# Splitting the context again in two stages instead of storing its high and low halves

## The chip, the cores and the metric

The kernel runs on one core of a Trainium2 chip. The metric is the device time of one execution in microseconds (us). TensorE (PE, with its weight loads shown as PEld), VectorE (DVE), ScalarE (ACT) and GpSimd (POOL) each take their instructions in order; SyncE (SP) issues every DMA of this kernel, also in order.

## The reference, cut to what matters

Four transformer layers run one after the other on `x` (32 batches of 112 tokens by 256 channels). Every layer attends from `x` to the same context `ctx_1024` (32 batches of 375 tokens by 256 channels). Layer 0 normalises the context first; layers 1, 2 and 3 project it raw:

```python
x = _L0_xattn_ref(x, ctx_1024, ...)             # cross attention, context rms-normalised
x = _L1_xattn_ref(x, ctx_1024, ...)             # self attention, cross attention, gated feed-forward, 8-bit rounding
    k = (ctx @ wk) ; v = (ctx @ wv)
x = _L2_xattn_ref(x, ctx_1024, ctx_1024, ...)   # cross attention, 16 heads of 64, feed-forward
    K = einsum('bsc,hdc->bhsd', k, Wk) ; V = einsum('bsc,hdc->bhsd', v, Wv)
x = _L3_xattn_ref(ctx_1024, x, ...)             # causal self attention, cross attention to x_e = ctx, feed-forward
    k = einsum('btc,hcd->bhtd', kv_in, wk) + bk ; v = ...
```

Everything is float32. The kernel gets float32 accuracy from faster matmuls by splitting an operand into a high half (rounded to the float32r type) and a low half (the rest), and adding three products: high by high, high by low, low by high.

## The kernel before, in words

**Stages.** The nine sweeps over the 32 batches are named layer and kind: `l0x`, `l1s`, `l1x`, `l1f`, `l2x`, `l2f`, `l3s`, `l3x`, `l3f` (s self, x cross, f feed-forward). They run in five stages: l0x beside l1s, l1x beside l1f, l2x alone, l2f beside l3s, l3x beside l3f. A batch is 8 slots long in l1x and l2x (one slot is two heads in l1x, and one pair of heads of one quarter in l2x) and 4 slots in l3s (four heads each); groups of two batches share the norm, the query projection and, in l3s, the keys.

**The order.** `run` writes the instructions out slot by slot. What belongs to a slot comes with a lag in slots (`LAGS`): in l2x the scores and softmax in the slot itself, the normalising of the probabilities one slot later, their transposes two, the product with the values three. What prepares a unit is an atom with a lead in slots (`LEAD`): an atom of cost 0 (a load, a split) is written when its slot comes, projections fill in by their cost. The compiler's scheduler then orders each engine's instructions from that list by a simulated time; on the chip each engine follows its own list in order, and waits where something is not ready.

**Buffers.** SBUF tiles come from pools with a fixed number of buffers: `k3` has 11, shared by raw context, values, probabilities, transposed probabilities, keys and projected halves; `k6` has 5, for the split context (high and low, 128 x 2 x 2 x 376) and, in l3s, for the keys read back.

**The context.** `ctx_atoms` (L530) serves l1x and l2x. In l1x, `load` (atom `cload`) takes a k3 tile, clears its last column on POOL (L540) and loads 375 KB of raw context (L541); `cut` takes a k6 tile and calls `split` (L228): a copy of 128x752 into the high half, on ACT or DVE in turn as `SHARE` says (L200, L202), and a subtraction on POOL into the low half (L231). As l1x is not the last sweep, `cut` then stores the two halves in DRAM (`cd`, 752 KB, L552). From then on `kept(b)` finds them: in l2x `load` does nothing and `cut` loads 752 KB from `cd` into a k6 tile (L547). In l3s, `kv_atoms` (L508) already projects the context with the weights of l3x: its `load` (atom `c2`, L516) loads 752 KB from `cd`, `qk_atoms` projects the keys, `v_atoms` the values, both with lead 1, and both go to DRAM (L842, L521) for l3x.

**What stands around it in SP's order.** l1x has four DMA transposes per batch (L1125), which turn the rounded probabilities for the matmuls of L1070. l2x loads values projected earlier (L750) and turns its queries by four DMAs (L681). l3s writes its queries and keys to DRAM (L868, L842) and reads them back spread out: two keys tiles (L852) and eight query DMAs per batch (L879), which the scores of L1158 wait for.

Of the kernel before, what the change touches and what calls it, by code (L numbers as in the profile page):

```python
# [8 lines left out]
F32 = mybir.dt.float32  # L9
F32R = mybir.dt.float32r  # L10
# [9 lines left out]
TE = 376  # L20
# [41 lines left out]
class Kern:  # L62
# [7 lines left out]
        l1x=[0, 1, 3, 6, 7],  # L70
        l1f=[0, 1, 5, 0, 3],
        l2x=[0, 1, 2, 3, 3],
        l2f=[0, 0, 0, 0, 0],
        l3s=[0, 0, 1, 2, 2],
# [6 lines left out]
        l1s=dict(load=5, stats=5, apply=3, q=2, k=2, v=1),  # L81
        l1x=dict(load=17, stats=12, apply=10, cload=14, cut=14, q=8, apart=[2, -1], k=4, v=-1, v2=[-2, -4, -6, -7], again=-7),
        l1f=dict(load=13, stats=11, apply=10, gate=2, gelu=1, again=-3),
        l2x=dict(load=10, stats=7, apply=6, cload=11, cut=7, q=4, k=[1, 1], v=0, vload=2),
        l2f=dict(load=6, stats=5, apply=3),
        l3s=dict(load=10, stats=8, apply=7, q=7, qload=3, k=6, v=3, c2=4, k2=1, v2=1),
        l3x=dict(load=16, stats=11, apply=10, cload=13, cut=12, q=9, qload=4, k=8, v=6, kload=8, vload=4),
        l3f=dict(load=6, stats=5, apply=2),
    )
# [152 lines left out]
    def vec(self, name, ncol):  # L242
# [12 lines left out]
        l3s="L3_xattn_m_proj_b", l3x="L3_xattn_c_proj_b", l3f="L3_xattn_f_b2",  # L255
# [218 lines left out]

        return [(L["load"], 0, load), (L["stats"], 0, stats), (L["apply"], gb * 200, apply)]

    def kept(self, b):
        return self.cd.get(b)

    def early_v(self, qd):  # L480

        return qd < self.EARLY and "l1x" in self.sweeps and "l2x" in self.sweeps
# [25 lines left out]
    def kv_atoms(self, s, b, wd, kb):  # L508

        nc = self.nc  # L510
        L = self.LEAD[s]
        st = {}

        def load():
            st["c"] = o = self.t([128, 2, 2, TE], F32R, "k6")
            nc.sync.dma_start(o.bitcast(F32), self.kept(b).bitcast(F32))  # L516

        def keep_v(v):
            d = self.v3[b] = self.dram([2, TB, 768], F32, f"v3_{b}", 1)
            for q in range(2):  # L520
                nc.sync.dma_start(d[q], v[q].rearrange("p a h d -> p (a h d)"))  # L521

        blocks = [(a * TB, TB) for a in range(3)]
        return (
            [(L["c2"], 0, load)]
            + self.qk_atoms(L["k2"], lambda: wd["k2"], lambda: lambda k, q: st["c"][:, k, q, :], TE, False, False, kb, None, f"k3_{b}", lambda d: self.k3.update({b: d}))
            + self.v_atoms(L["v2"], lambda: wd["v2"], lambda k, q, a: st["c"][:, k, q, a * TB : (a + 1) * TB], blocks, None, None, keep_v)
        )

    def ctx_atoms(self, s, b, c):  # L530


        nc = self.nc
        L = self.LEAD[s]

        def load():
            if self.kept(b) is not None:
                return
            c["raw"] = raw = self.t([128, 2, TE], F32, "k3")
            nc.gpsimd.memset(raw[:, :, T:TE], 0.0)  # L540
            nc.sync.dma_start(raw[:, :, :T], self.A["ctxT"][b].rearrange("(k p) t -> p k t", p=128))  # L541

        def cut():
            c["c"] = o = self.t([128, 2, 2, TE], F32R, "k6")
            d = self.kept(b)
            if d is not None:
                nc.sync.dma_start(o.bitcast(F32), d.bitcast(F32))  # L547
                return
            self.split(c["raw"], o[:, :, 0, :], o[:, :, 1, :], ("ctx", "crest"))
            if s != self.sweeps[-1]:  # L550
                d = self.dram([128, 2, 2, TE], F32R, f"cd{b}", 1)
                nc.sync.dma_start(d.bitcast(F32), o.bitcast(F32))  # L552
                self.cd[b] = d

        return [(L["cload"], 0, load), (L["cut"], 0, cut)]

    def ctx_norm_atoms(self, s, b, g, c):

# [802 lines left out]
    OVER = dict(l2x=0.0, l3x=34.0)  # L1361

    def run(self):
        self.xd, self.cd, self.vd, self.k3, self.v3, self.mark = {}, {}, {}, {}, {}, {}
        ws = {s: self.weights(s) for s in self.sweeps}
        units = {}
        for s in self.sweeps:
# [24 lines left out]
        for s in self.sweeps:  # L1392
            n, at = 0, []
            for u in units[s]:
                for q, (lead, cost, f) in enumerate(u.atoms):
                    m = n - lead
                    d = mine[s][m] if 0 <= m < len(mine[s]) else mine[s][0] + m if m < 0 else mine[s][-1] + m - len(mine[s]) + 1
# [84 lines left out]
        for k in range(max(max(due), len(slots)) + 1):  # L1482
# [7 lines left out]
            if k < len(slots):  # L1490
                s, ui, sl = slots[k]
# [18 lines left out]
            for q in range(1, 5):  # L1510
                for j in [j for e, j in due.get(k, []) if e == q]:
                    self.cur = slots[j][0]
                    f = slots[j][2].st[q]
# [81 lines left out]
```

## Time and profile before

| what | value |
|---|---|
| median of 3 runs | 4973.1 us (4965.27 to 4977.62) |
| the profiled execution's own time | 4961.83 us |
| its span in the trace | 4960.0 us |
| l0x and l1s | about 0 to 1116 us |
| l1x and l1f | about 1116 to 2232 us |
| l2x | about 2232 to 3348 us |
| l2f and l3s, with the changes of stage around them | about 3348 to 4216 us |
| l3x and l3f | about 4216 to 4960 us |
| stores of halves (cd<-k), all in l1x | 32 of 752 KB |
| loads of halves (k<-cd), 32 in l2x and 32 in l3s | 64 of 752 KB |
| loads of raw context, all in l1x | 32 of 375 KB |

In the profile, L12 is line 12 of the kernel; `k` stands for any tile of the pools k3, k6 and ki, and buffer numbers are left out. An idle time carries the name of what ended it ("<-DMA k<-cd": a load from cd landed). "PEclk" or "granted clock" is the share of TensorE's clock that the chip granted. A line of `copy` or `split` is shared by many callers, so the shape tells which one it is: 128x752 is the context.

### The profile page before, as it was taken

To read this page: it belongs to the slowest core of one execution; us is meant where nothing else is said; L and a number is where in the kernel's file an instruction comes from. 1 tells how busy PE (TensorE), PEld (TensorE's weight loads), DVE (VectorE), ACT (ScalarE), POOL (GpSimd) and SP (SyncE) were. 2 spreads that over 40 slices of the span, in tenths; PEclk is the share of its full clock that TensorE was granted. 3 is DMA by queue.
4 is the path that set the end of the run, shared out by engine and by line. 5 is a ranking of instruction groups with operands and counts; after the bars stand their busy time and mean duration, and the time that the engine had idled before them with its cause. 6 is when DMAs were issued, how large, how long until landed. Compare 5 with 4: busy or idle time off the path is not lost.

```text
span 4960.0 us, 111607 instructions
## 1 busy us (share of the span) xinstructions
PE 4515.7 (91%) x37824; PEld 4007.3 (81%) x37824; DVE 3631.7 (73%) x9806; ACT 3417.2 (69%) x10644; POOL 2110.2 (43%) x3674
## 2 busy tenths in 40 slices
PE   6999999998779888888999999998999986899999
PEld 5888888886668777777999999998888875788888
DVE  4788888888887777776688888886555554777776
ACT  4788888887777776675577777774555544677776
POOL 4455555555443333332233333334333332556655
PEclk9999999999889999999999999999999997999999
DMA  4433333335676666676454555443665666666662
GB/s 102 124 84 86 84 81 84 86 84 132 138 148 134 131 134 134 132 147 132 112 142 143 143 143 143 142 132 109 206 192 177 205 191 192 171 159 160 161 160 77
DMA packets 585414, 674.53 MB, mean 136 GB/s; under 512 B 318688, under 2 KB 495056, under 8 KB 584656
## 3 DMA queue, kind: packets, MB, share of 16 engines
q1 hardware_dynamic: 584848, 667.40, 53.3%
q8 instruction: 305, 5.00, 0.4%
q14 instruction: 261, 2.14, 0.1%
HBM read 323.55 MB, written 173.02 MB: 100 GB/s over the span
## 4 chain that ended last, share of the span: by engine, by line
PE 39%; DMA 7%; DVE 4%; ACT 1%; SPq 1%; issue 1%; POOL 1%; ACTq 0%; DVEq 0%; POOLq 0%
PE ps L664 6%; PE ps L235 5%; PE ps L236 4%; PE ps L237 4%; PE sc L773 3%; PE ps L795 3%; PE ps L1070 3%; DMA qs<-dq_l3s 2%; PE sc L1106 2%; PE acc L235 1%; PE acc L237 1%; DMA k<-cd 1%; PE acc L236 1%; PE ps L1233 1%; PE acc L1273 1%
## 5 line engine op out<-in xcount | busy, mean ns | idle before, releaser
L217 POOL TENSOR_SCALAR k<-k,sm 112x375 f32<-112x375 f32 (+1 forms) x1536 | 928.7, 617 | 1051.7 <-DVE sm L646 475.9
L200 ACT ACTIVATE k<-ps 125x336 f32<-125x336 f32 (+4 forms) x2005 | 912.4, 468 | 418.8 <-PE ps L237 194.9
L606 DVE TENSOR_REDUCE sm<-sc 112x1 f32<-112x375 f32 x1792 | 947.0, 540 | 177.0 <-PE sc L773 88.9
L612 ACT ACTIVATE k<-sc,sm 112x375 f32<-112x375 f32 x1536 | 878.2, 577 | 106.7 <-DVE sm L606 86.6
L664 PE MATMUL ps<-ident,k 112*125 112x112 f32 x4608 | 730.2, 276 | 17.4 <-issue 4.2
L664 PEld LDWEIGHTS ps<-ident,k 112*125 112x125 f32 x4608 | 649.0, 189 | 69.9 <-issue 36.3
L773 PE MATMUL sc<-k,qs 128*112 128x376 f32 x2048 | 540.9, 357 | 18.0 <-ACT k L612 9.0
L235 PE MATMUL ps<-w,k 128*125 128x256 f32 (+2 forms) x1344 | 433.4, 322 | 33.1 <-ACT k L612 17.5
L235 PE MATMUL ps<-h,w 128*128 128x224 f32 x1408 | 409.4, 297 | 42.5 <-DVE h L202 15.9
L695 DVE TENSOR_TENSOR k<-ps,k 64x376 fp32r<-64x376 f32 x640 | 350.1, 547 | 121.5 <-ACT k L200 106.2
L236 PE MATMUL ps<-h,w 128*128 128x224 f32 x1408 | 393.4, 282 | 0.5 <-DVE h L231 0.5
L202 DVE COPY k<-ps 125x336 f32<-125x336 f32 (+2 forms) x619 | 289.2, 467 | 141.2 <-PE ps L237 71.7
L237 PE MATMUL ps<-h,w 128*128 128x224 f32 x1408 | 391.5, 281 | 0.0
L236 PE MATMUL ps<-w,k 128*125 128x256 f32 (+2 forms) x1344 | 389.6, 290 | 0.0
L237 PE MATMUL ps<-w,k 128*125 128x256 f32 (+2 forms) x1344 | 388.9, 289 | 0.0
L235 PE MATMUL ps<-k,w 128*128 128x376 f32 x896 | 343.8, 384 | 41.6 <-DMA k<-cd 28.7
L213 POOL TENSOR_SCALAR k<-k,sm 112x375 f32<-112x375 f32 x256 | 164.4, 642 | 448.4 <-DVE sm L646 279.4
L795 PE MATMUL ps<-k,k 125*64 125x112 f32 (+1 forms) x4608 | 350.7, 296 | 2.1 <-ACT k L200 1.3
L773 PEld LDWEIGHTS sc<-k,qs 128*112 128x112 f32 x2048 | 304.8, 177 | 47.0 <-ACT k L612 23.6
L235 PEld LDWEIGHTS ps<-h,w 128*128 128x128 f32 x1408 | 272.3, 196 | 69.7 <-issue 20.2
L235 PEld LDWEIGHTS ps<-w,k 128*125 128x125 f32 (+2 forms) x1344 | 263.5, 196 | 73.6 <-ACT k L612 28.2
L612 ACT ACTIVATION_READ_ACCUMULATOR k<-sc,sm 112x1 f32 x1536 | 321.1, 209 | 0.0
(213 smaller groups left out, 12642.2 us busy)
## 6 DMA issues: line engine op xcount, KB each, us to landing
qs<-h SPq DMA_DIRECT2D x512, 224.0 KB
k<-k SPq DMA_DIRECT2D x192, 376.0 KB
k<-cd SPq DMA_DIRECT2D x64, 752.0 KB
vd<-k SPq DMA_DIRECT2D x128, 375.0 KB
k<-vd SPq DMA_DIRECT2D x128, 375.0 KB
qs<-dq_l3s SPq DMA_DIRECT2D x256, 112.0 KB
qs<-dq_l3x SPq DMA_DIRECT2D x256, 112.0 KB
x<-xd SPq DMA_DIRECT2D x224, 112.0 KB
```

What stands on the lines that cost most here:

```text
L200: self.nc.scalar.activation(out, in_, AF.Identity)
L202: self.nc.vector.tensor_copy(out, in_)
L217: self.nc.gpsimd.tensor_scalar(out, in_, by, 1.0, ALU.mult, ALU.mult)
L235: mm(out, lhs(0), rhs(0), start=start, stop=False)
L236: mm(out, lhs(0), rhs(1), start=False, stop=False)
L237: mm(out, lhs(1), rhs(0), start=False, stop=stop)
L606: nc.vector.tensor_reduce(nms[j], sc[j][:, :n], AX.X, ALU.max, negate=True)
L612: nc.scalar.activation(p[:, j, :n], sc[j][:, :n], AF.Exp, bias=nms[j], scale=1.0 if scale is None else scale, accum_out=sm[:, j : j + 1])
L664: self.nc.tensor.transpose(pst[:TB, a * S : (a + 1) * S], p[:, j, a * TB : (a + 1) * TB], self.ident[:S, :S])
L695: nc.vector.tensor_tensor(ks[o, j, :], pk[r, :TE], ks[r, j, :].bitcast(F32), ALU.subtract)
L773: nc.tensor.matmul(sc[:, :TE], qs[:, hd, q, bs], kk, start=q == 0, stop=q == 1)
L795: nc.tensor.matmul(o if gqa else o[:, mm, :], vq[:, a, hd * 64 : hd * 64 + 64], st["pt"][:, :, j, ta] if gqa else st["pt", mm][:, j, ta], ...
```

## The change

The halves are no longer stored. `kept` and the dictionary `cd` go. `ctx_atoms` always loads raw context and always splits it; it now takes the names of its two leads, and `kv_atoms` in l3s uses it in place of its own load. So l1x loses its store; l2x and l3s each load 375 KB into a k3 tile in place of 752 KB into a k6 tile, and split it. In l2x the load moves from lead 7 (there it was part of `cut`) to lead 9 and the split has lead 7; in l3s the load moves from lead 4 to lead 5 and the split has lead 4. The copy into the high half is on ACT in l2x, on ACT and DVE in turn in l3s; the subtraction is on POOL in both.

```diff
-        l2x=dict(load=10, stats=7, apply=6, cload=11, cut=7, q=4, k=[1, 1], v=0, vload=2),
+        l2x=dict(load=10, stats=7, apply=6, cload=9, cut=7, q=4, k=[1, 1], v=0, vload=2),
-        l3s=dict(load=10, stats=8, apply=7, q=7, qload=3, k=6, v=3, c2=4, k2=1, v2=1),
+        l3s=dict(load=10, stats=8, apply=7, q=7, qload=3, k=6, v=3, c2=5, cut2=4, k2=1, v2=1),
...
-        ("l1x", "ctx"): (1, 1, 0),
+        ("l1x", "ctx"): (1, 1, 0), ("l2x", "ctx"): (1, 0, 0), ("l3s", "ctx"): (1, 1, 0),
...
-    def kept(self, b):
-        return self.cd.get(b)
...
     def kv_atoms(self, s, b, wd, kb):
...
-        def load():
-            st["c"] = o = self.t([128, 2, 2, TE], F32R, "k6")
-            nc.sync.dma_start(o.bitcast(F32), self.kept(b).bitcast(F32))
...
         return (
-            [(L["c2"], 0, load)]
+            self.ctx_atoms(s, b, st, ("c2", "cut2"))
             + self.qk_atoms(L["k2"], ...)
             + self.v_atoms(L["v2"], ...)
         )
-    def ctx_atoms(self, s, b, c):
+    def ctx_atoms(self, s, b, c, leads=("cload", "cut")):
...
         def load():
-            if self.kept(b) is not None:
-                return
             c["raw"] = raw = self.t([128, 2, TE], F32, "k3")
             nc.gpsimd.memset(raw[:, :, T:TE], 0.0)
             nc.sync.dma_start(raw[:, :, :T], self.A["ctxT"][b].rearrange("(k p) t -> p k t", p=128))

         def cut():
             c["c"] = o = self.t([128, 2, 2, TE], F32R, "k6")
-            d = self.kept(b)
-            if d is not None:
-                nc.sync.dma_start(o.bitcast(F32), d.bitcast(F32))
-                return
             self.split(c["raw"], o[:, :, 0, :], o[:, :, 1, :], ("ctx", "crest"))
-            if s != self.sweeps[-1]:
-                d = self.dram([128, 2, 2, TE], F32R, f"cd{b}", 1)
-                nc.sync.dma_start(d.bitcast(F32), o.bitcast(F32))
-                self.cd[b] = d
-
-        return [(L["cload"], 0, load), (L["cut"], 0, cut)]
+
+        return [(L[leads[0]], 0, load), (L[leads[1]], 0, cut)]
```

More of the change, by code (lines that the diff above doesn't have):

```diff
@@ L1363, in run @@
     def run(self):
-        self.xd, self.cd, self.vd, self.k3, self.v3, self.mark = {}, {}, {}, {}, {}, {}
+        self.xd, self.vd, self.k3, self.v3, self.mark = {}, {}, {}, {}, {}
         ws = {s: self.weights(s) for s in self.sweeps}
```

## The prediction

> **What bounds the kernel now.** I read the busy times by stage first, then the waits inside the three stages that the change touches, then the order of time around their DMAs. The table by stage (span, then busy time of PE, PEld, DVE, ACT and POOL, granted clock, DMA share, GB/s):
>
> ```profile
> 1116.00:2232.00 1116.00, 939.05 (x7027) 812.48 (x7024) 888.22 (x2462) 795.46 (x2243) 442.62 (x720) 0.93 0.67 137
> 2480.00:3348.00 868.00, 864.29 (x7691) 816.03 (x7690) 712.66 (x1665) 628.01 (x1782) 281.41 (x477) 1.00 0.50 141
> 3472.00:4216.00 744.00, 646.46 (x5319) 582.29 (x5317) 394.31 (x1092) 371.44 (x1510) 267.06 (x459) 0.92 0.63 194
> ```
>
> PE bounds l2x: 3.7 us idle in 868, at full clock. In l1x (first line) it is idle for 177 of 1116 us and in l3s (third) for 98 of 744, both at a lower clock and with more DMA. So work taken from the DMAs can pay in l1x and l3s, and nothing but PE's own work counts in l2x.
>
> l3s, in order of time: SP around one group's loads, and PE's first matmul after them; then its waits in the stage.
>
> ```profile
> 3620.05 1.53 SPq L516 DMA_DIRECT2D k<-cd  x1
> 3621.64 3.59 SPq L879 DMA_DIRECT2D qs<-dq_l3s  x4
> 3625.32 0.49 SPq L516 DMA_DIRECT2D k<-cd  x1
> 3626.75 12.53 SPq L879 DMA_DIRECT2D qs<-dq_l3s  x8
> 3634.16 0.65 PE L235 MATMUL ps<-k,w 128*128 128x376 f32 x1 [5.95 <-DMA k<-cd]
> ...
> PE sc L1158 <- DMA qs<-dq_l3s: 35.0, 13, 7.9
> PE ps L235 <- DMA k<-cd: 26.6, 6, 9.4
> ...
> SPq L879 <- DMA k<-cd: 49.9, 24, 2.8
> ```
>
> Two kept loads and 12 query loads go out in one burst of 2 x 752 + 12 x 112 = 2848 KB, and PE waits for its last pieces. In the timeline of PE this comes once per group of two batches, some 46 us apart: 13 waits from 3540 to 4098 us, of 1.29, 4.37, 5.95, 0.99, 2.05, 3.53, 3.62, 2.58, 3.03, 1.46, 4.75, 3.90 and 9.37 us, 46.9 us in all. Each ends 11.9 to 16.0 us after one kept load was issued and 7.5 to 11.4 us after the next; 4 end on `cd`, 9 on query loads behind it. SP is itself held at L879 until `cd` loads have landed.
>
> The clock after such a wait (same columns as the table):
>
> ```profile
> 3634.10:3637.60 3.50, 3.44 (x16) 2.53 (x16) 1.19 (x4) 0.00 (x0) 0.00 (x0) 0.50 0.71 200
> 3637.60:3641.10 3.50, 3.50 (x19) 3.50 (x18) 2.79 (x10) 0.00 (x0) 0.00 (x0) 0.50 0.38 114
> ...
> 1865.00:1868.50 3.50, 3.46 (x22) 3.09 (x22) 1.61 (x4) 1.80 (x6) 0.00 (x0) 0.54 1.77 196
> ```
>
> The clock is halved for 3.5 to 7 us after a wait of 2 to 6 us, so a wait costs about 1.7 us more than its length (3.5 x 0.5).
>
> l1x, one batch in order of time:
>
> ```profile
> 1858.00 4.26 SPq L1125 DMA_TRANSPOSE k<-k  x1
> 1859.08 1.80 POOL L231 TENSOR_TENSOR k<-k,k 128x752 fp32r<-128x752 f32 x1 [2.04 <-DVE sm L646]
> 1862.32 0.73 SPq L552 DMA_DIRECT2D cd<-k  x1
> 1865.04 0.47 PE L1070 MATMUL ps<-k,k 128*32 128x112 bf16 x12 [2.09 <-DMA k<-k]
> ```
>
> The store of the halves goes out 0.06 us after a transpose has been issued, and PE waits for that transpose. Of PE's 70 us of waits on transposes from 1240 to 2232 us, 50.4 us (24 waits, 2.1 us each) have a store between the transpose and its use; the 18 others are 1.1 us each. From the end of the transpose's issue to its use it is 3.54 us with a store, 3.01 us without.
>
> Prices of what is added, from l1x, where all of it runs already:
>
> ```profile
> L231 POOL TENSOR_TENSOR k<-k,k 128x752 fp32r<-128x752 f32 x32 | 59.3, 1852 | 54.7 <-DVE sm L646 22.5 <-ACT k L200 18.7 <-DVE k L202 13.5
> L200 ACT ACTIVATE k<-k x16: 818/831/865, 1111.5 to 2178.8; 128x752 fp32r<-128x752 f32 x16
> L540 POOL MEMSET k<- 128x2 f32 x31 | 5.3, 172 | 0.8 <-DMA k<-k 0.8
> ```
>
> The DVE copy of the same shape takes 0.55 us.
>
> **The change part by part.** *l1x loses 32 stores.* SP gets back 0.68 us of issue each, off the path: SP waits at most of its instructions. On the path is the delay of the transpose in flight. By landing times it is 0.53 us x 24 = 13 us; by the sizes of the waits, 1.0 us x 24 = 24 us. I take 18 us between them. At worst it is 0, if what makes those transposes late is the split on POOL before them, which stays; at best all 50 us, and 20 of clock. The split itself and L541 do not change.
>
> *l2x loads raw context and splits it.* Per batch POOL gets 1.85 + 0.17 us and ACT 0.83 us in about 34 us of a batch; they are busy 281 and 628 of 868 us there. What covers it is the lag of one slot, some 4.3 us, between normalising on POOL and the transposes on PE, against a delay of at most 2.0 us. The load is off the path: issue to copy is 3.2 to 8.3 us in l1x, against two slots (8.6 us) between the leads. Two things are queued behind: on POOL, the normalising (L217) behind the clearing and the subtraction; on ACT, the exponentials and key copies behind the copy. New is a buffer: raw context holds one of 11 k3 buffers for some two slots, and l2x's value loads already wait for one (SP at L750 for scores, 170.6 us in 62 waits). A value load has six slots before its use, so I take 0.25 us per batch, 8 us. Ends: a gain of at most 4 us (PE's idle time); a loss of all that is added in a row, 2.85 us x 32 = 91 us, if there is no cover. I stay near the low end as the nearest row is PE's 3.7 us of idle beside POOL's hundreds. SP's own waits at L547 (113.5 us, for a free k6 buffer) go; nothing late hangs on them.
>
> *l3s loads raw context and splits it.* The burst shrinks to 2 x 375 + 12 x 112 = 2094 KB, 26% less; 14 us of it are 3.7 us less. Each of the 13 waits loses that, or all it has: 37 us. Nine of them vanish and take their slow clock along: 9 x 1.7 = 15 us. Together 52 us. What is late next is the projection's own list: PE fills 86% of the stage, and the gaps that remain are of 1 us (on L202 and L926). Ends: 24 us, if only the waits on `cd` go (23.7 us); 47 + 13 x 1.7 + 8 = 77 us, if all go with some at the stage's end. Added are 0.83 us on ACT or 0.55 us on DVE, and 2.02 us on POOL per batch of 23 us, where they are busy 371, 394 and 267 of 744 us. The copy now waits in order for its load, with softmaxes queued behind it on ACT and normalisings on POOL. In l1x, where load and split have the same lead, that costs 13 us in 31 loads (8.6 on DVE, 4.6 on ACT); here a slot lies between. I take 0.2 us per batch on the path, 6 us. Ends: 0, and 2.5 us x 32 = 81 us with no cover.
>
> The sum is -18 + 8 - 52 + 6 = -56 us: 4961.8 becomes 4906 for the profiled execution. That one is 11.3 us below the median of the runs; from the median, 4973.1 becomes 4917 us.
>
> **Two rules of the Trainium skill.** For the loads, the row is 11.9 to 14.1 us from issue to use of a kept half against 3.2 to 8.3 us for raw context. "DMA: Bandwidth & Descriptors" (Anatomy of one DMA) gives about 2.0 us plus bytes by 436 GB/s, measured on the other descriptor path: by it a load would fall only from 3.8 to 2.9 us, and the l3s part would be worth 32 x 0.9 = 28 us rather than 52. For the clock, the row is a granted clock of 0.54 after a wait of 2.09 us. "TensorE: Matmul & The Clock Gate" (Part 1) has the clock fall only after an idle window of about 3.4 us: by it, short waits would cost no clock, and of the 15 us only the two vanishing waits of over 3.4 us would count, 3 us.
>
> **The rivals.** *The wait is handed on.* The query loads and the value stores keep the burst's length (SP is held at L879 for 64.9 us by v<-k, more than by `cd`), so l3s gains 12 us, l1x nothing, and the 14 us added remain: 4973 + 2 = 4975. For it: 9 of 13 waits end on queries. Against it: all 13 come with two kept loads.
>
> *l2x starves for k3 buffers.* Raw context takes a buffer, probabilities and keys wait, and PE, which has no idle time to give, loses the full 2.85 us per batch: 4973 - 18 - 52 + 91 + 6 = 5000. It makes the kernel no faster from 2.0 us of stall per batch on (64 us) and slower by the bound from 2.5. For it: the value loads' waits. Against it: these loads are early by design, and a k3 buffer comes free every 1.2 us or so (3.5 k3 tiles per slot of 4.3 us).
>
> *ACT and DVE wait for late raw loads in l3s.* SP stays late and a load takes 12 us; the copy stands a slot (5.8 us) behind, holds its engine for 6 us, and a quarter of that reaches PE in place of today's waits: 32 x 1.6 = 51 us, 4973 - 18 + 8 + 51 = 5014. Against it: a landing of about 4 us in l1x at a higher DMA share.
>
> *The burst dissolves.* The load goes out a slot earlier, all of the 77 us come, and l1x gives 40 with clock: 4973 - 77 - 40 + 8 + 6 = 4870.
>
> **How the numbers follow.** Chances: forecast 0.60, handed on 0.15, starved 0.13, late loads 0.07, dissolved 0.05. The forecast's own range is 4885 to 4950. Reaching to the other cases, 4868 to 4995 leaves out half of each extreme. A measurement tells 0.3%, 15 us, from no change. Faster: 0.60 + 0.05 + a fifth of the handed-on case = 0.68; the rest of that case 0.12; slower 0.20.
>
> **What would show it.** No cd<-k and no k<-cd; 96 raw loads of 375 KB; 96 subtractions of 128x752 on POOL. In l3s PE's waits on query loads below 20 us in all, none over 4 us on context, and a clock above 0.95 over the stage. In l1x, PE's waits on transposes at 45 to 57 us. In l2x PE idle below 15 us. It is wrong if l2x is longer by more than 20 us, if ACT, DVE or POOL show long waits on in_ctxT in l3s, or if the once-per-group wait stays with its size.

## The result and the profile after

The changed kernel takes 5019.07 us (median of 6 runs, 5015.54 to 5020.8), the kernel before 4975.36 us beside it (6 runs, 4965.27 to 4981.68). The ratio is 1.0074, with a 95% interval of 1.0057 to 1.009: slower, where the prediction said 4917 us and faster. The profiled execution has a span of 5017.5 us, that of before 4960.0.

The first and last value stores (vd<-k) and l3s's query loads (qs<-dq_l3s) mark the stages in SP's order of time, in every kernel of this study. l1x is from the first vd<-k to the last, l2x from there to the first qs<-dq_l3s, l3s from there to the last row of them (a row can hold several loads, and its start counts). Each stage time is of one profiled execution, and executions differ: beside e5 to e8, the kernel before took 4962 to 5010 us.

| us | to l1x | l1x | l2x | l3s | rest | span |
|---|---|---|---|---|---|---|
| before | 1168.4 | 1143.0 | 1132.7 | 743.5 | 772.4 | 4960.0 |
| after | 1172.8 | 1158.0 | 1155.2 | 754.3 | 777.2 | 5017.5 |

Of the 57.5 us, 15.0 lie in l1x, 22.5 in l2x and 10.8 in l3s. The 15 of l1x are within its spread. Seven experiments below have l1x as before had it, and take 1159.3, 1163.7, 1157.0, 1153.6, 1157.3, 1146.5 and 1157.8 us for it; with the 1143.0 of before, the shortest, the mean is 1154.8. Five have l1x as after has it, and take 1148.2, 1158.7, 1159.8, 1164.4 and 1154.4 us; with the 1158.0 of after the mean is 1157.3. The medians of the runs are 43.7 us apart: l2x and l3s make up 33 of them, and the rest has no place in these profiles.

The table by stage of the changed kernel (span, then busy time of PE, PEld, DVE, ACT and POOL, granted clock, DMA share, GB/s); the second and third stretch are moved by 30 and 38 us against those shown of before, roughly as the work is:

```profile
1116.00:2232.00 1116.00, 934.42 (x6976) 804.79 (x6975) 881.29 (x2445) 789.24 (x2226) 438.30 (x717) 0.92 0.58 112
2510.00:3378.00 868.00, 849.80 (x7495) 795.02 (x7495) 705.83 (x1621) 632.01 (x1762) 328.06 (x520) 1.00 0.47 127
3510.00:4254.00 744.00, 644.40 (x5227) 576.49 (x5226) 405.99 (x1087) 373.06 (x1496) 315.62 (x511) 0.92 0.58 175
```

The DMAs did get lighter: 0.67 to 0.58 in l1x, 0.63 to 0.58 in l3s. PE got nothing for it. In l2x it does 7495 matmuls in 868 us where it did 7691, and is idle for 18.2 us instead of 3.7.

*l1x.* PE's waits on transposes, 70.4 us (41 waits) before from 1240 to 2250 us, are nearly what they were (over the whole stage 78.6 us before and 79.0 after):

```profile
PE ps L1052 <- DMA k<-k: 68.3, 37, 8.0
```

*l2x.* ACT's waits (total, times, longest) from 2510 to 3378 us:

```profile
ACT k L200 <- DMA k<-in_ctxT_dram: 30.9, 22, 2.9
```

and one of them in order of time, on SP, ACT and POOL:

```profile
2967.40 0.93 SPq L531 DMA_DIRECT2D k<-in_ctxT_dram  x1
...
2972.78 0.83 ACT L200 ACTIVATE k<-k 128x752 fp32r<-128x752 f32 x1 [1.95 <-DMA k<-in_ctxT_dram]
2973.52 0.52 ACT L211 ACTIVATE xh<-ps,vec_L_xattn_ln_b,vec_L_xattn_ln_w 128x224 f32<-128x224 f32 x1
...
2973.69 1.78 POOL L231 TENSOR_TENSOR k<-k,k 128x752 fp32r<-128x752 f32 x1 [1.37 <-ACT k L200]
```

The load goes out 5.4 us ahead of its copy and lands just then. ACT stands for 1.95 us, the scaling of xh (L211) behind it is late, and POOL waits too. Further down the line PE waits for what DVE makes of that xh, a wait that before did not have, and the longest in total of PE's 18.2 us of idle time:

```profile
PE ps L777 <- DVE xh L213: 5.3, 5, 1.8
```

SP issues the load late because the k3 tile comes late: it waits at L531 for the matmuls (L777) that give a tile back.

```profile
SPq L531 <- PE ps L777: 40.9, 14, 3.4
```

*l3s.* One group in order of time, on SP, DVE, POOL, ACT and PE:

```profile
3964.20 0.46 SPq L531 DMA_DIRECT2D k<-in_ctxT_dram  x1
...
3969.35 0.55 DVE L202 CAST k<-k 128x752 fp32r<-128x752 f32 x1 [5.56 <-DMA k<-in_ctxT_dram]
...
3969.98 1.77 POOL L231 TENSOR_TENSOR k<-k,k 128x752 fp32r<-128x752 f32 x1 [5.76 <-DVE k L202]
...
3970.16 0.28 ACT L200 ACTIVATE k<-ps 125x128 f32<-125x128 f32 x1 [4.50 <-DVE k L202]
3970.33 0.54 ACT L200 ACTIVATE pp<-ps 112x448 f32<-112x448 f32 x1
...
3970.92 0.84 PE L1052 MATMUL ps<-pp,s 112*32 112x112 f32 x8 [3.10 <-ACT pp L200]
```

The six lines are one chain. The load lands 5.15 us after its issue. DVE stands before the copy in order; a part of the value projection is to be copied behind it; ACT, which copies the next part into the same tile, waits for DVE; the probabilities (pp) are queued behind that on ACT; PE waits for the probabilities. Over the stage, from 3520 to 4160 us:

```profile
PE ps L1052 <- ACT pp L200: 21.4, 12, 3.5
PE sc L1140 <- DMA qs<-dq_l3s: 21.1, 11, 3.5
ACT k L200 <- DMA k<-in_ctxT_dram: 31.9, 12, 4.8
DVE k L202 <- DMA k<-in_ctxT_dram: 33.4, 12, 5.6
```

PE's 23.7 us of waits on `cd` are gone, and 21.4 us of waits on ACT have come. In l3s SP hardly waits for a tile (0.3 us at L531): there the load is late by its place in SP's order, not by its buffer. In the whole kernel the splits number what was forecast (columns: busy, mean ns, then the idle time ahead and what ended it):

```profile
L231 POOL TENSOR_TENSOR k<-k,k 128x752 fp32r<-128x752 f32 x96 | 174.1, 1814 | 218.9 <-ACT k L200 120.5 <-DVE k L202 58.3 <-DVE sm L628 24.8
L200 ACT ACTIVATE k<-k 128x752 fp32r<-128x752 f32 x64 | 53.2, 832 | 78.6 <-DMA k<-in_ctxT_dram 72.7 <-POOL k L217 2.5 <-DMA k<-dk 2.1
L202 DVE CAST k<-k 128x752 fp32r<-128x752 f32 x32 | 17.5, 547 | 48.3 <-DMA k<-in_ctxT_dram 48.3
```

The prices of the added work were right (1.81, 0.83 and 0.55 us); the 121 us that ACT and DVE stand before it were not in the sum, but for the 13 us of them that l1x had already.

### The profile page after: what moved, and what is told of

Same layout as the page of the kernel before. It is cut to its first block, busy times and chain, and to the rows that moved or that the text cites. A ratio compares the mean times of both kernels' runs of the same rounds, so it can differ in the third digit from the quotient of the medians.

```text
span 5017.5 us, 111863 instructions
## 1 busy us (share of the span) xinstructions
PE 4543.0 (91%) x37824; PEld 4012.5 (80%) x37824; DVE 3666.7 (73%) x9822; ACT 3450.2 (69%) x10692; POOL 2227.0 (44%) x3802
## 4 chain that ended last, share of the span: by engine, by line
PE 37%; DMA 9%; DVE 4%; ACT 2%; SPq 1%; issue 1%; POOL 1%; ACTq 0%; DVEq 0%; POOLq 0%
PE ps L646 6%; PE ps L235 5%; PE ps L236 4%; PE ps L237 4%; DMA k<-in_ctxT_dram 3%; PE ps L1052 3%; PE ps L777 3%; PE sc L755 3%; PE sc L1088 2%; DMA qs<-dq_l3s 2%; PE acc L237 1%; PE acc L235 1%; PE acc L236 1%; DMA k<-k 1%; PE ps L1215 1%
## 5 line engine op out<-in xcount | busy, mean ns | idle before, releaser
L235 PE MATMUL ps<-h,w 128*128 128x224 f32 x1408 | 411.8, 299 | 43.7 <-DVE h L202 15.8
L777 PE MATMUL ps<-k,k 125*64 125x112 f32 (+1 forms) x4608 | 350.7, 296 | 9.0 <-DVE xh L213 5.3
L235 PEld LDWEIGHTS ps<-h,w 128*128 128x128 f32 x1408 | 273.6, 197 | 71.0 <-issue 21.4
```

Source lines behind the costliest of these rows:

```text
L235: mm(out, lhs(0), rhs(0), start=start, stop=False)
L777: nc.tensor.matmul(o if gqa else o[:, mm, :], vq[:, a, hd * 64 : hd * 64 + 64], st["pt"][:, :, j, ta] if gqa else st["pt", mm][:, j, ta], ...
```

## The experiments

Each ratio is to the kernel before beside it on the same chip; from one comparison to the next that kernel's own median went from 4975 to 4991 us. "Lead" is how many slots ahead of its use a step stands.

### Which part of the change costs

Theory at this point: a wait for raw context was handed to the engines that copy it, in l2x above all. Rivals: l3s alone, or the missing stores, or the work of the split.

**One store only (e1).** The kernel before with the store for batch 0 alone:

```diff
-            if s != self.sweeps[-1]:
-                d = self.dram([128, 2, 2, TE], F32R, f"cd{b}", 1)
-                nc.sync.dma_start(d.bitcast(F32), o.bitcast(F32))
-                self.cd[b] = d
+            if b == 0:
+                self.cd0 = self.dram([128, 2, 2, TE], F32R, "cd0", 1)
+                nc.sync.dma_start(self.cd0.bitcast(F32), o.bitcast(F32))
+            self.cd[b] = self.cd0
```

> The kernel before, but only the first batch's halves are stored and both later stages load that one tile 32 times each: 31 stores of 752 KB leave l1x, every load stays. (The context of batch 0 stands in for all, so the output differs; the work does not.) If the store delays the transposes, as predicted, l1x is about 18 us shorter: 4957 us against 4975. If the transposes are late by themselves, the time stays within 5 us of before and PE's waits on transposes stay near 70 us.

Measured: 4983.02 us, ratio 1.0004 (0.9989 to 1.0019). PE waits 67.3 us (35) on transposes from 1240 to 2250 us, and 75.6 over the whole stage. The stores are worth nothing that can be measured: at most some 5 us by the interval, not 18.

**l2x alone (e2), l3s alone (e3).** The kernel before with raw loads and splits in one of the two stages; the other keeps its load of halves.

In l2x alone:

```diff
-        l2x=dict(load=10, stats=7, apply=6, cload=11, cut=7, q=4, k=[1, 1], v=0, vload=2),
+        l2x=dict(load=10, stats=7, apply=6, cload=9, cut=7, q=4, k=[1, 1], v=0, vload=2),
...
-            if self.kept(b) is not None:
-                return
...
-            d = self.kept(b)
-            if d is not None:
-                nc.sync.dma_start(o.bitcast(F32), d.bitcast(F32))
-                return
...
-            if s != self.sweeps[-1]:
+            if s == "l1x":
```

> The kernel before, with the raw load and the split in l2x alone; l1x still stores, l3s still loads the halves. If copies and subtractions that wait in order for a late raw load stop PE in l2x, this costs 20 to 25 us there (4995 to 5000 us), with ACT waiting some 30 us for the load and PE idle some 18 us from 2510 to 3380 us. If l2x pays only what was predicted, +8 us. If the loss at the end of l1x (about 15 us) comes from what l2x hoists ahead, it is here too: 5010 us.

Measured: 5012.26 us, ratio 1.0065 (1.0043 to 1.0086); l2x takes 1155.2 us, as in after, with ACT waiting 31.3 us for raw context and PE idle for 17.1 from 2500 to 3368 us. So the 20 to 25 us that were expected in l2x are there. The total, 32 us (21 to 43), is larger than expected, near the 5010 of the last reading, in which l2x lengthens the end of l1x. l1x, 1159.3 us, does not speak for that reading: with l2x as before it takes 1163.7 us in e3 and 1157.0 in e12. What is left of the total is not placed.

In l3s alone:

```diff
-        l3s=dict(load=10, stats=8, apply=7, q=7, qload=3, k=6, v=3, c2=4, k2=1, v2=1),
+        l3s=dict(load=10, stats=8, apply=7, q=7, qload=3, k=6, v=3, c2=5, cut2=4, k2=1, v2=1),
...
-            [(L["c2"], 0, load)]
+            self.ctx_atoms(s, b, st, ("c2", "cut2"))
...
-            if self.kept(b) is not None:
+            if s == "l2x":
                 return
...
-            if d is not None:
+            if s == "l2x":
                 nc.sync.dma_start(o.bitcast(F32), d.bitcast(F32))
                 return
...
-            if s != self.sweeps[-1]:
+            if s == "l1x":
```

> The kernel before, with the raw load and the split in l3s alone; l1x stores, l2x loads the halves. If the once-per-group wait is handed from PE to ACT and DVE, l3s is 5 to 15 us longer: 4980 to 4990 us, with 60 us of ACT and DVE waits on the raw load. If the smaller load shortens the burst as predicted, 46 us are gained: 4929 us.

Measured: 4982.32 us, ratio 1.0007 (0.9994 to 1.0021); l3s takes 758.4 us in the profiled execution, the slowest of the ten, with ACT and DVE waiting 63.0 us for raw context (expected: 60). Nearly all of the loss is l2x's, and l3s gains nothing.

**The changed kernel, with 32 stores put back (e4)** that nobody reads:

```diff
             self.split(c["raw"], o[:, :, 0, :], o[:, :, 1, :], ("ctx", "crest"))
+            if s == "l1x":
+                d = self.dram([128, 2, 2, TE], F32R, f"cd{b}", 1)
+                nc.sync.dma_start(d.bitcast(F32), o.bitcast(F32))
```

> The changed kernel with the 32 stores of halves put back into l1x, where nobody reads them. If removing the store gained something that was lost elsewhere, this is 13 to 24 us slower than the changed kernel: 5032 to 5043 us. If it gained nothing, within 5 us of 5019.

Measured: 5007.08 us, ratio 1.0047 (1.0031 to 1.0063). It is not slower than the changed kernel, whose interval overlaps: no 13 to 24 us were gained by leaving the stores out.

### l2x: work, wait or buffer

**No wait of the copy for the load (e5).** In the changed kernel, l2x splits a resident tile in place of raw context.

```diff
-            self.split(c["raw"], o[:, :, 0, :], o[:, :, 1, :], ("ctx", "crest"))
+            raw, hi, lo = c["raw"], o[:, :, 0, :], o[:, :, 1, :]
+            if s == "l2x":
+                raw = self.biases[:, : TE // 2].bitcast(F32).unsqueeze(1).to_broadcast([128, 4, TE // 2])
+                hi, lo = (z.rearrange("p k (e t) -> p k e t", e=2) for z in (hi, lo))
+                raw = raw.rearrange("p (k e) t -> p k e t", k=2)
+            self.split(raw, hi, lo, ("ctx", "crest"))
```

> The changed kernel, but in l2x the copy and the subtraction read a resident tile (the first 188 columns of the biases, four times over) instead of the raw context. The raw loads, their k3 buffers, the clearing on POOL, the copy on ACT and the subtraction on POOL all stay; only the wait of the copy for its load goes. l2x's cross attention is thus computed from wrong context. Three theories. (W) ACT stands in order before the copy until the load has landed (30 us in 22 waits from 2500 to 3300 us), and what is queued behind is late for DVE and PE: then the ratio to the kernel before is 0.999 to 1.002, and from the last vd<-k to the first qs<-dq_l3s it takes 1132 to 1138 us as before, not the 1155 of the changed kernel. (K) The k3 buffer that raw context holds is what starves the rest: nothing changes, 1.006 to 1.008. (E) It is the added 0.83 us on ACT and 1.9 us on POOL per batch: nothing changes, 1.006 to 1.008.

Measured: 5003.59 us, ratio 1.0036 (1.0019 to 1.0053); l2x takes 1146.9 us. Neither W nor K alone: 8 of the 22 us go with the wait of the copy. The edit does more than was meant: as nobody reads raw context, its tile comes free when the load lands, and whoever has the tile next waits for that. From 2500 to 3368 us these waits are 15.9 us in 14 times, on exponentials (L599) and key copies; one of the rows:

```profile
ACT k L599 <- DMA k<-in_ctxT_dram: 4.7, 4, 2.0
```

So part of the wait is handed to the tile's next users, and SP still waits 38.4 us at L531 for the matmuls that give a tile back, as in after. The 8 us are no clean price of the copy's wait.

**A later split (e6).** The changed kernel with one number changed:

```diff
-        l2x=dict(load=10, stats=7, apply=6, cload=9, cut=7, q=4, k=[1, 1], v=0, vload=2),
+        l2x=dict(load=10, stats=7, apply=6, cload=9, cut=4, q=4, k=[1, 1], v=0, vload=2),
```

> The changed kernel, but in l2x the split stands three slots (some 13 us) later than it did (lead 4 instead of 7); the load stays. (W) A load lands 4 to 6 us after its issue, so the copy no longer waits: 1.000 to 1.003. (K) Raw context holds its k3 buffer for five slots instead of two, more than twice as long: 1.010 or more. (E) 1.006 to 1.008, as the work is the same; a little more if the projection now waits for the split.

Measured: 5037.92 us, ratio 1.0101 (1.0066 to 1.0136); l2x takes 1175.6 us. This speaks for K: another 20 us, and exponentials that write probabilities into k3 tiles now wait for the matmuls that give one back, a wait that neither before nor after has (from 2530 to 3398 us):

```profile
ACT k L594 <- PE ps L777: 22.0, 71, 0.8
```

What I had not foreseen: ACT still waits 29.2 us for raw context in the same stretch, as its load, too, goes out later, 3.0 to 4.8 us ahead of the copy in the loads between 2700 and 2850 us. So the time from load to copy did not grow, and SP waits 56.6 us at L531 for a tile, where it waited 40.9. Moving the copy away from the load does not help while the load waits for its tile.

**A buffer of its own (e7), and what a buffer costs (e8).** In the changed kernel, raw context of l2x and l3s gets one 3 KB buffer, at the price of one of the 11 in k3; beside it, before with ten:

```diff
-    BUFS = dict(w=8, x=11, xh=4, ki=6, s1=9, sm=32, ot=7, pp2=4, k3=11, h=3, qs=2, k6=5)
+    BUFS = dict(w=8, x=11, xh=4, ki=6, s1=9, sm=32, ot=7, pp2=4, k3=10, h=3, qs=2, k6=5, craw=1)
...
-        l2x=dict(load=10, stats=7, apply=6, cload=9, cut=7, q=4, k=[1, 1], v=0, vload=2),
+        l2x=dict(load=10, stats=7, apply=6, cload=12, cut=7, q=4, k=[1, 1], v=0, vload=2),
...
-        l3s=dict(load=10, stats=8, apply=7, q=7, qload=3, k=6, v=3, c2=5, cut2=4, k2=1, v2=1),
+        l3s=dict(load=10, stats=8, apply=7, q=7, qload=3, k=6, v=3, c2=7, cut2=4, k2=1, v2=1),
...
-            c["raw"] = raw = self.t([128, 2, TE], F32, "k3")
+            c["raw"] = raw = self.t([128, 2, TE], F32, "k3" if s == "l1x" else "craw")
```

In e8, `k3=10` is the whole edit.

> The changed kernel, but raw context of l2x and l3s has one buffer of its own, taken from the k3 ring (10 instead of 11), and its loads stand three slots earlier in l2x and two in l3s. A load can be issued as soon as the split of the batch before is done, some 30 us ahead. (W) No copy waits for a load in either stage; l2x falls back to 1132 to 1138 us and l3s loses ACT's and DVE's 65 us of waits, of which a fifth reached PE: 0.996 to 1.001. (K) One k3 buffer less for the rest all the time, instead of a buffer held for two slots of eight: 1.007 to 1.015. (E) 1.005 to 1.008.

> The kernel before with 10 k3 buffers instead of 11, nothing else: what a k3 buffer is worth. (W) and (E): 0.999 to 1.003. (K): 1.004 or more, with l2x (from the last vd<-k to the first qs<-dq_l3s) longer by 10 us or more.

Measured: e7 5048.14 us, ratio 1.0124 (1.0087 to 1.016); e8 5051.48 us, ratio 1.0125 (1.0089 to 1.0161). Read by their totals both would be K's. By stage they are not: with ten buffers, the kernel before takes 1217.0 us in l1x (74 more than the 1143.0 of before, 62 more than the mean of 1154.8) and 1135.1 us in l2x (2 more). The table by stage of e8:

```profile
1116.00:2232.00 1116.00, 908.53 (x6607) 778.82 (x6604) 826.03 (x2324) 751.59 (x2116) 423.04 (x686) 0.90 0.61 128
2540.00:3408.00 868.00, 863.50 (x7674) 815.59 (x7675) 713.30 (x1659) 638.22 (x1780) 278.98 (x475) 1.00 0.50 141
```

So the eleventh buffer is l1x's, and l2x does not need it. With its own buffer (e7) l2x takes 1137.3 us with raw context, load, copy and subtraction all there. That is against E, the work, and against the number of buffers as the cause. What is left is the tile's place among the k3 requests (the buffers of a pool are handed out in turn, as a ring): raw context waits for its turn, is loaded late, and holds its tile meanwhile. In l3s e7 missed: 755.2 us, with DVE waiting 87.3 us in 14 waits for raw context from 3550 to 4190 us. Two more slots of lead and one buffer do not take that wait away.

**Another ring (e9).** If so, the five k6 buffers should do, which held the loads of halves before; the edit is to the changed kernel:

```diff
-        l2x=dict(load=10, stats=7, apply=6, cload=9, cut=7, q=4, k=[1, 1], v=0, vload=2),
+        l2x=dict(load=10, stats=7, apply=6, cload=12, cut=7, q=4, k=[1, 1], v=0, vload=2),
...
-            c["raw"] = raw = self.t([128, 2, TE], F32, "k3")
+            c["raw"] = raw = self.t([128, 2, TE], F32, "k6" if s == "l2x" else "k3")
```

> The changed kernel, but l2x takes the buffer for raw context from the k6 ring (five of 6 KB, the ring that the kernel before used for the kept load) instead of the k3 ring, and the load stands three slots earlier (lead 12 instead of 9). l1x and l3s stay as changed; the split, its engines and its place stay too. Since ten k3 buffers cost l2x nothing with the kept load, the number of buffers can't be what l2x lost; the theory is now (T) that buffers of a ring are handed out in turn, so raw context that waits for its turn is issued late, stops ACT at the copy, and while it is held stops the next one whose turn it is: in the k6 ring l2x takes 1132 to 1140 us (from the last vd<-k to the first qs<-dq_l3s) and the whole 1.000 to 1.004 of before. (E) If the work of the split or the clearing were the cost after all: 1150 us or more, 1.006 to 1.008.

Measured: 4989.7 us, ratio 1.0021 (1.0008 to 1.0033); l2x takes 1134.8 us. Loads go out 9.8 us or more ahead of the copy, ACT has no wait for them, and PE is idle for 4.4 us:

```profile
2490.00:3358.00 868.00, 863.60 (x7677) 813.51 (x7676) 709.00 (x1660) 645.83 (x1804) 329.41 (x527) 1.00 0.47 129
```

All of l2x's loss is gone, with the same work done in the same place. T's numbers hold for l2x. The edit has two parts, another ring and a load three slots earlier, as e7's has too. The earlier load in k3 was not run in l2x, so which of the two parts is needed is not shown.

**The same for l1x**, where k3 is short: raw context in k6, in the kernel before (e10) and in the changed one together with l2x (e11).

```diff
-            c["raw"] = raw = self.t([128, 2, TE], F32, "k3")
+            c["raw"] = raw = self.t([128, 2, TE], F32, "k6")
```

In e11 the tag is "k6" for l1x and l2x and "k3" for l3s, and l2x has `cload=12`.

> The kernel before (halves stored in l1x and loaded in l2x and l3s), but raw context in l1x, its one stage with raw context, has a k6 buffer instead of a k3 buffer. (T) With ten k3 buffers l1x took 74 us longer (1217 instead of 1143 us from the first to the last vd<-k), so k3 is short there, and a ring without the raw tile in it should give some of it back: l1x shorter by 5 to 25 us, 0.995 to 0.999. Rival: l1x needs the buffers of k6 as much, or what it is short of is something that the eleventh buffer already settles: 1.000 to 1.005.

> The changed kernel with raw context of l1x and l2x in k6 buffers, and l3s as changed: both edits at once. (T) 0.996 to 1.002. If l3s by itself loses 10 us, as the profiles of the other runs had it, nearer to the upper end. (E) 1.004 to 1.008.

Measured: e10 5003.88 us, ratio 1.0053 (1.0036 to 1.007), l1x 1188.5 us; e11 4999.84 us, ratio 1.004 (1.0025 to 1.0056). Both are misses of T. l2x keeps its gain in e11 (1136.3 us), and l1x takes 1167.5 us. The rival, that l1x needs its k6 buffers as much, fits; which wait costs the time in l1x was not shown.

### l3s: bytes or time

**Nothing waits for context (e12).** Before with raw loads in l3s (as e3), where the split reads a resident tile, with the edit of e5 for `s == "l3s"`.

> The kernel before with raw loads in l3s alone, where the copy and the subtraction read a resident tile (188 columns of the biases, four times over) instead of raw context, so that l3s's own context is wrong and nothing in l3s waits for it; loads, buffers and the work of the split stay. (H) If the wait for the burst was handed from PE to ACT, DVE and POOL, which stand in order before the copy, taking it away brings what the prediction hoped for: l3s (first to last qs<-dq_l3s) shorter by 25 us or more against the 743 to 758 us of the others, 0.991 to 0.996. (N) If the raw load is only one of several things that are late in the same place, query loads and values for instance: 735 us or more, 0.997 to 1.002.

Measured: 4949.26 us, ratio 0.9942 (0.9921 to 0.9962); l3s takes 717.2 us. H: the gain is there, and the wait of ACT and DVE ate it. PE's waits on queries, which were to shrink with the bytes, are larger than the 33.9 us of before in the same stretch (3480 to 4160 us), not smaller:

```profile
PE sc L1159 <- DMA qs<-dq_l3s: 41.2, 15, 6.5
```

**Real context, loaded earlier (e13, e14).** As e3, with the load at lead 9 and at lead 12:

```diff
-        l3s=dict(load=10, stats=8, apply=7, q=7, qload=3, k=6, v=3, c2=5, cut2=4, k2=1, v2=1),
+        l3s=dict(load=10, stats=8, apply=7, q=7, qload=3, k=6, v=3, c2=9, cut2=4, k2=1, v2=1),
```

(`c2=12` in e14.)

> The kernel before with raw context in l3s alone, split where the change splits it, but loaded four slots earlier (lead 9 instead of 5). In the runs so far the load went out behind SP's stores and loads for the queries, 4 to 6 us before its copy, and the copy's engine stood until it landed; without that wait l3s was 26 us shorter and the ratio 0.9942. (H) An early load takes the wait away with right context: first to last qs<-dq_l3s in 715 to 730 us, 0.992 to 0.997. (N) It waits for its k3 buffer in turn, goes out as late as before and holds up what stands behind it in the ring: 743 to 770 us, 1.000 to 1.008.

> The same with lead 12: raw context holds its k3 buffer for eight slots instead of one. (H) As with lead 9, if buffers are plenty in l3s (ten did no harm there): 0.992 to 0.997. (N) Worse than lead 9, by the long hold: 1.003 or more.

Measured: e13 4963.9 us, ratio 0.996 (0.9946 to 0.9974), l3s 731.2 us; e14 4955.89 us, ratio 0.9943 (0.9923 to 0.9963), l3s 727.2 us. In e13 DVE still waits 17.0 us for raw context (from 3490 to 4130 us), in e14 neither ACT nor DVE does; PE's largest waits in e14 are

```profile
PE sc L1154 <- DMA qs<-dq_l3s: 27.8, 12, 5.0
PE sc L1154 <- issue: 9.5, 2, 5.5
PE sc L1154 <- DMA v<-k: 7.9, 2, 4.4
```

**Both causes mended in the changed kernel**: e9's l2x, and `c2=9` (e15) or `c2=12` (e16) in l3s.

> The changed kernel (no stores of the halves) with l2x's raw context in a k6 buffer, loaded three slots earlier, and l3s's raw context loaded four slots earlier: both causes mended, context never stored. If the two stages add up, 0.994 to 0.999: as e13 in l3s, as before in l2x. If l3s's early load is no use, 1.001 to 1.005, as with the k6 buffer alone.

> The changed kernel with l2x's raw context in a k6 buffer and l3s's raw context loaded at lead 12: no halves stored, and both causes mended as far as the runs know how. Adding up: l2x as before, l3s 16 us shorter than before, l1x unchanged: 0.994 to 0.998. It ties with the kernel that leaves l1x and l2x alone (0.9943 [0.9923, 0.9963]) unless the store that is gone is worth something after all.

Measured: e15 4972.39 us, ratio 0.9971 (0.9957 to 0.9985), l2x 1136.2 and l3s 730.3 us; e16 4960.57 us, ratio 0.9963 (0.9944 to 0.9981), 1133.2 and 724.1 us. With both mended the loss is gone in both stages. The whole change, mended, is no faster than the early load in l3s alone (e14), so that stores and l2x's bytes once more show no worth.

**The halves, loaded earlier (e17, e18).** The kernel before with one number changed:

```diff
-        l3s=dict(load=10, stats=8, apply=7, q=7, qload=3, k=6, v=3, c2=4, k2=1, v2=1),
+        l3s=dict(load=10, stats=8, apply=7, q=7, qload=3, k=6, v=3, c2=12, k2=1, v2=1),
```

(`c2=6` in e18.)

> The kernel before, its kept load in l3s eight slots earlier (lead 12 instead of 4), nothing else: halves are stored and loaded as before. (R) If the gain of the early raw load is its own (half the bytes, the burst smaller), the kept load gains less or nothing: 0.997 or more, first to last qs<-dq_l3s 738 us or more. (L) If it is only that the load left the once-per-group burst, the kept load gains as much: 0.992 to 0.997, and the change was never needed for it.

> The same with lead 6. (R) 0.998 or more. (L) 0.993 to 0.999; (either) if the k6 ring of five is what limits how early a kept load can go, as its buffers are 6 KB, this is no worse than lead 12.

Measured: e17 4955.8 us, ratio 0.9949 (0.9933 to 0.9964), l3s 727.5 us; e18 4960.93 us, ratio 0.9954 (0.9936 to 0.9972), l3s 740.9 us in the profiled execution. L, not R: 752 KB loaded early are as good as 375 KB loaded early. PE's waits on `cd`, 25.1 us before from 3480 to 4160 us, are gone in e17 with the DMA share of the stage where it was (second line; before had 0.62). Its waits on query loads, 33.9 us before, are not:

```profile
PE sc L1158 <- DMA qs<-dq_l3s: 36.8, 14, 7.0
...
3480.00:4160.00 680.00, 607.78 (x5020) 550.29 (x5020) 363.97 (x1030) 348.18 (x1418) 254.91 (x435) 0.93 0.63 196
```

So there are versions that beat both kernels, the one before by 0.4 to 0.6%, in three kernels whose intervals overlap (e14, e16, e17), and the simplest of them leaves the change out and moves one load.

## Why the prediction was wrong

**"l1x loses 32 stores": -18 us, measured 0.** The 0.53 us by which transposes with a store in flight are later was a correlation. Take the stores out (e1) and PE still waits 62.5 us on transposes from 1240 to 2232 us (69.7 before), against the 45 to 57 us that were to be seen; over the whole stage it is 75.6 against 78.6 us. The low end, 0, was the right value. Nor does the stage's time follow these waits: with ten k3 buffers (e8) they fall to 53.4 us over the stage while l1x gets 62 to 74 us longer, with other waits in their place.

**"l2x loads raw context and splits it": +8 us, measured +22.** The prices of the work were right. The step that failed is "The load is off the path", for which the prediction gave the two slots (8.6 us) between the leads. A lead says where a step stands in the written order, not when its transfer starts: the load got its k3 tile late and went out 3.9 to 5.7 us before the copy wherever ACT waited. Landing times of 3.2 to 8.3 us, read in l1x, had said that this would be too little. The rival of the starved buffers had the right resource, but not by its number: ten buffers are enough in l2x (e8), and what hurts is a tile that must be asked for in turn and held over a transfer. Of the 22 us, 8 go when the copy no longer waits (e5). That the other 14 are the tile's turn and hold is the reading of e5, e6, e7 and e9 together. It is argued and not shown: an earlier load in the same ring was not tried, and which instruction pays in the changed kernel stays open, but for PE's 5.3 us on xh.

**"The burst shrinks": -52 us, with the 6 us of the copy -46 for the stage, measured +11.** Mean l3s over before, e1, e2, e8 and e10, which load halves at lead 4, is 743.8 us; over after, e3, e4, e5, e6, e9 and e11, with raw loads at lead 5, it is 755.2 us. The runs are kinder to it than the traces: e3's ratio allows a loss of 10 us at most. The step that failed took the length of the burst, 2848 KB, as the cause of PE's wait, so that fewer bytes would end it sooner. e17 moves all its bytes and has no wait on `cd`; e12 moves fewer and has more of the waits on queries. What the stage gained by was the moment at which the context is loaded: moved to lead 12, that load brings it from 743.8 to 727 us at either size. The waits on query loads, 9 of the 13 waits of the prediction, remain in e17 (36.8 us against 33.9), and why those loads are late stays open. A small slip in the sum: eight of the 13 waits, not nine, are of 3.7 us or less, so the term for the clock was 14 us and not 15.

**"The copy now waits in order for its load": +6 us.** Here the mechanism was named and mispriced by its cover ("here a slot lies between"). The lead of 5 against 4 does not help: where the copy waited, its load had gone out 3.6 to 6.7 us before it and landed just then, so a slot of 5.8 us is no more than a landing takes. In the rival "ACT and DVE wait for late raw loads in l3s" a quarter of 6 us per batch reaches PE, for 51 us; the chain shown above is that rival's, at a smaller price: ACT and DVE stand for 65.3 us in 24 waits, and PE for 21.4 us. That rival's total, 5014 us, is within 0.1% of the 5019 measured, but by the wrong stage: it had the loss in l3s, where a third of it lies, and l2x at 8. "The wait is handed on" (4975) had l1x right, at nothing, and named the handing on, but to other DMAs.

**What was to be seen.** 96 raw loads and 96 subtractions: yes. Waits on query loads in l3s below 20 us: 21.1. No wait of PE over 4 us on context in l3s: none at all. A clock above 0.95 over the stage: 0.92, as before. PE idle below 15 us in l2x: 18.2. Two of the three signs of a wrong prediction are what the profile shows: l2x longer by more than 20 us, and long waits of ACT and DVE on raw context in l3s (POOL waits for their copies).

**The two rules weighed.** Where the copy waited in l2x, it took 3.9 to 5.7 us from the issue of a load of 375 KB to its landing. The fit of the Trainium skill, "DMA: Bandwidth & Descriptors" (Anatomy of one DMA), which is of the other descriptor path, gives an estimate of 2.9 us; these loads took longer. Neither that rule's 28 us nor my 52 came, as both priced bytes, and e17 has the gain with all of them.

For the clock: after PE's wait of 3.10 us, which ends at 3970.92 us, the granted clock is about half for some 7 us:

```profile
3963.00:3967.00 4.00, 4.00 (x37) 4.00 (x36) 0.79 (x2) 0.86 (x3) 1.22 (x2) 1.00 0.64 160
3970.50:3974.00 3.50, 3.08 (x19) 2.69 (x20) 1.76 (x5) 3.50 (x16) 2.48 (x3) 0.58 0.27 59
3974.00:3978.00 4.00, 4.00 (x24) 3.42 (x23) 2.68 (x7) 1.87 (x10) 1.42 (x4) 0.51 0.31 112
3978.00:3982.00 4.00, 3.68 (x31) 3.38 (x30) 3.10 (x9) 1.97 (x9) 2.67 (x4) 1.00 0.10 37
```

By an estimate from these rows, 3.50 x 0.42 + 4.00 x 0.49 = 3.4 us are lost beyond the wait, twice the 1.7 us that the prediction took. The Trainium skill, "TensorE: Matmul & The Clock Gate" (Part 1), names an idle window of about 3.4 us ahead of the half clock; here a shorter wait was enough.

## What to carry to other kernels

A wait at the consumer does not say whether the transfer is too large or too late; move its issue earlier before making it smaller, and read issue-to-use times against landing times in the trace. Work that is put between a load and its consumer moves the wait to an engine that runs in order, and everything queued there pays it, so a cheap copy of 0.55 us can hold three engines for 5 us. A step's lead covers a load only if its buffer is free that early: ask which ring the buffer comes from and who holds it, stage by stage, since one ring can be short in one stage (62 to 74 us for one buffer in l1x) and have room in the next (2 us in l2x).

## What was not expected of the hardware

Nine points of DMA share in l1x (0.67 to 0.58) and some 24 MB less of stores left l1x as long as it was. In l3s half the bytes of context, and five points of share (0.63 to 0.58), gave nothing that the full size did not give as well once it was loaded early (727.5 us in e17, 727.2 in e14). In this kernel the moment of issue decided, and the bytes beside it did not.
